# Mixture-of-experts tail of a decoder block: the remaining rows of up to 64 per expert dealt two experts to a tile

## The chip, the cores and the metric

The kernel runs on one core of one Trainium2 chip. A time is the device time of one execution in microseconds (us). The kernel before was run three times: 970.29, 963.82 and 967.57 us, median 967.57. One more execution was profiled; it took 964.87 us, and its span, from the first to the last instruction, is 963.1 us. All durations below come from that execution. Everything is in float32. In the trace, one float32 matrix product stands as two records (two passes over the array), and so does each of its weight loads.

## The reference, cut to what matters

The block is cross-attention followed by a mixture of experts, on 8 x 256 = 2048 tokens of 512 numbers. Only the second half matters here:

```python
h = layernorm(x).reshape(-1, 512)                      # 2048 tokens
scores = softmax(h @ gate_weight.T)                    # 8 experts
topk_w, topk_i = _group_limited_topk(scores)           # best 2 groups of 4, then 2 experts per token
wmat = (one_hot(topk_i, 8) * topk_w[..., None]).sum(1)
g = einsum('th,nfh->ntf', h, gate_w)                   # F = 352
u = einsum('th,nfh->ntf', h, up_w)
e = einsum('ntf,nhf->nth', silu(g) * u, down_w)
routed = einsum('nth,tn->th', e, wmat)
shared = (silu(h @ sh_gate_w.T) * (h @ sh_up_w.T)) @ sh_down_w.T     # F = 704
out = x + routed + shared
```

Each token goes to two of eight experts, so 4096 rows are to be computed by experts. The inputs are fixed by a seed. Evaluated on them, the reference gives the experts 473, 523, 552, 459, 702, 517, 475 and 395 rows.

## The kernel before

Attention, the router and the shared expert are interleaved in `attention` by a hand-written order (`order`, and stages in `Others` that fill the gaps). The PE, ACT, DVE and SP instructions run in exactly the order in which the program issues them; GpSimd's (POOL) order is chosen by a scheduler. For each batch, `router` gives every (token, expert) pair a place in the DRAM table `rows`, and `send` (L961) scatters the normalised tokens there, together with the token's scores and its number. Expert `e` owns the table's rows from `e * S_R` on, with `S_R` = 2176.

After the last batch, `plan` (L969 to L1033) works out on DVE, from the counts, which tiles of 128 rows the experts need. It is 27 DVE instructions, issued back to back. `t_end` (where each expert's rows end) comes first; `t_row` (first row of a tile), `t_exp` (its expert), `t_one` (one-hot of it) and `t_all` (number of tiles) come last. While `plan` runs, PE works through the shared expert of the last batch (`Shared.pieces`, L156). There a result tile `gu` is in one of the three buffers of the PSUM pool `ps_m` (L99), ACT computes the tanh (L176), and two DVE instructions (L177, L178) finish it and release the buffer.

`routed` then computes the experts. The weights of all eight stay in SBUF (`wgu_all`, `wd_all`; 1408 and 768 KB for one expert), loaded by DMAs on SP's queue in the first steps. Tile `i` goes through these functions:

- `load` (L363): SP reads the tile's first row from `t_row` (for `i` >= 8) and starts a DMA of 128 rows into `xs`, which has three buffers.
- `turn` (L368): PE turns the rows with four transposes (`rx`, L372), ACT copies them to `rxT` (L374), DVE picks the weight `rw` and the token numbers `rid` (L376 to L384).
- `up` (L386): PE reads the expert's number from `t_exp` and makes 8 products (`rg`, L393), four for the gate and four for the up projection, each 128 rows of weights by 352 columns; ACT applies silu (L401), DVE multiplies (L403).
- `turn_act` (L405): three transposes (`ra`, L409), two DVE copies to `raT`.
- `down` (L414): 3 products of 512 columns (`ro`, L420), a DVE scaling to `ry` (L428; three buffers), and a scatter by GpSimd that adds the rows to the output (L429).

`run` (L459) is software-pipelined. Step `i` issues load(i + 2), the weights of expert i + 3 while there are any, turn(i + 1), up(i), down(i - 1) and turn_act(i).

Tiles 0 to 7 are the first 128 rows of each expert. For the rest an expert gets whole tiles of 128 rows, the last one partly empty: with the counts above 3, 4, 4, 3, 5, 4, 3 and 3, in sum 29. `N_TILE` = 39 is the most that any routing needs; `N_RUN` = 37 tiles are always computed, so all of 8 + 29 = 37 are filled, and two more stand behind a branch (L485) that is taken if `t_all` says so. Before the experts read their tiles, 8 DMAs write an empty tile (`blank`, L448) behind each expert's last row.

Of the kernel before, what the change touches and what calls it, by code (L numbers as in the profile page):

```python
# [35 lines left out]
F32 = mybir.dt.float32  # L38
I32 = mybir.dt.int32
# [23 lines left out]
S_R = NT + P  # L63
N_TILE = TOP_K * NT // P - 1 + N_EXP
N_RUN = N_TILE - 2
N_PLAN = N_TILE - N_EXP
W = 528
# [9 lines left out]
def xattn_ffn(  # L77
# [35 lines left out]

    blank = dram.tile([P, W], F32, name="blank")
    rows = dram.tile([N_EXP * S_R + P, W], F32, name="rows")
# [217 lines left out]
def routed(ctx, tc, ps_m, wgu, wd, ident, rows, t_exp, t_row, t_one, t_all, t_end, blank, out, tail, right):  # L333
# [11 lines left out]

    def value(table, i, engine, top):
        return nc.values_load(
            table[0:1, i : i + 1],
            engines=(engine,),
            min_val=0,  # L350
            max_val=top,
            skip_runtime_bounds_check_because=because,
        )
# [9 lines left out]
    def load(i):  # L363
        first = i * S_R if i < N_EXP else value(t_row, i - N_EXP, ENG.SP, N_EXP * S_R)
        xs[i] = early.tile([P, W], F32, tag="xs", bufs=3, name=f"xs{i}")
        nc.sync.dma_start(xs[i], rows[bass.ds(first, P), :])

    def turn(i):  # L368
        row = xs.pop(i)
        ps = ps_m.tile([P, NC, P], F32, tag="m", name=f"rx{i}")  # L370
        for c in range(NC):
            nc.tensor.transpose(ps[:, c], row[:, c * P : (c + 1) * P], ident)  # L372
        xTs[i] = early.tile([P, NC, P], F32, tag="xT", name=f"rxT{i}")
        nc.scalar.copy(xTs[i], ps)  # L374

        w1s[i] = early.tile([P, 1], F32, tag="w1", bufs=5, name=f"rw1_{i}")  # L376
        if i < N_EXP:
            nc.vector.tensor_copy(w1s[i], row[:, D + i : D + i + 1])
        else:
            wt = early.tile([P, N_EXP], F32, tag="wt", name=f"rw{i}")  # L380
            nc.vector.tensor_mul(wt, row[:, D : D + N_EXP], t_one[:, i - N_EXP])
            nc.vector.tensor_reduce(w1s[i], wt, AX.X, ALU.add)
        ids[i] = early.tile([P, 1], I32, tag="id", bufs=6, name=f"rid{i}")
        nc.vector.tensor_copy(ids[i], row[:, W_ID : W_ID + 1].bitcast(I32))  # L384

    def up(i):  # L386
# [3 lines left out]
        for k in range(2):  # L390
            for c in range(NC):
                w = wgu_all[:, bass.ds(e, 1), c, k * F : (k + 1) * F]
                nc.tensor.matmul(  # L393
                    gu[k],
                    lhsT=xT[:, c],
                    rhs=w.rearrange("p o f -> p (o f)"),
                    start=(c == 0),
                    stop=(c == NC - 1),
                )
        sg = work.tile([P, F], F32, tag="sg", name=f"rsg{i}")  # L400
# [13 lines left out]
    def down(i):  # L414
        e = exps.pop(i)
        o = ps_y.tile([P, D], F32, tag="y", name=f"ro{i}")
        aT = aTs.pop(i)
        for fc, (_, fn) in enumerate(FCH):
            w = wd_all[:fn, bass.ds(e, 1), fc]
            nc.tensor.matmul(  # L420
                o,
                lhsT=aT[:fn, fc],
                rhs=w.rearrange("p o d -> p (o d)"),
                start=(fc == 0),
                stop=(fc == len(FCH) - 1),
            )
        y = work.tile([P, D], F32, tag="y", bufs=3, name=f"ry{i}")
        nc.vector.tensor_scalar(y, o, w1s.pop(i), None, ALU.mult)  # L428
        nc.gpsimd.indirect_dma_start(  # L429
            out=out,  # L430
            out_offset=bass.IndirectOffsetOnAxis(ap=ids.pop(i), axis=0),
            in_=y,
            in_offset=None,
            compute_op=ALU.add,
        )

# [9 lines left out]
    for e in range(N_EXP):  # L446
        to = value(t_end, e, ENG.SP, N_EXP * S_R)
        alone(tc, nc.sync.dma_start(rows[bass.ds(to, P), :], blank).ins)  # L448
    while tail.cost < 0.8 * tail.total:
        tail.step()  # L450
    turn(0)
    while not tail.over:
# [3 lines left out]
        tc.tile_pool(name="rwork", bufs=2, side="right", reuse_waits="tile")  # L456
    )

    def run(tiles):  # L459

        a, n = tiles[0], tiles[-1] + 1
        for i in range(a, n + 1):
            if a + 3 <= i + 2 < n:
                load(i + 2)
            if i + 3 < N_EXP:
                up_weights(i + 3)
                down_weights(i + 3)
            if i + 1 < n:
                turn(i + 1)
            if i < n:  # L470
                up(i)
            if a < i:
                down(i - 1)
            if i < n:
                turn_act(i)

    run(range(N_RUN))

    filled = nc.values_load(
        t_all[0:1, 0:1],  # L480
        min_val=0,
        max_val=N_PLAN,
        skip_runtime_bounds_check_because=because,
    )
    with tc.If(filled > N_RUN - N_EXP):  # L485
        for i in range(N_RUN, min(N_RUN + 3, N_TILE)):
            load(i)
        turn(N_RUN)
        run(range(N_RUN, N_TILE))


def attention(
# [36 lines left out]
    first = late.tile([P, N_EXP], F32, name="first")  # L529
    nc.vector.tensor_copy(first, numbers[:, :N_EXP])  # L530

    count = late.tile([P, N_EXP], F32, name="count")
# [436 lines left out]
    def plan():  # L969


        behind = late.tile([P, N_EXP], F32, name="behind")
        nc.vector.tensor_add(behind, count, first)
        nc.vector.tensor_copy(t_end, behind)
        n16 = late.tile([P, NTT], F32, name="n16")
        nc.vector.tensor_copy(n16, numbers[:, N_EXP:])
        nc.vector.tensor_scalar(n16, n16, n16[:, 0:1], float(P), ALU.subtract, ALU.add)
        yield 0, False, 0, True

        shape = [P, N_EXP, NTT]  # L980
# [3 lines left out]
            count.unsqueeze(2).to_broadcast(shape),  # L984
            n16.unsqueeze(1).to_broadcast(shape),
            ALU.is_gt,
        )
        tiles = late.tile([P, N_EXP], F32, name="tiles")
        nc.vector.tensor_reduce(tiles, more, AX.X, ALU.add)

        shape = [P, N_EXP, N_EXP]
        upto = late.tile(shape, F32, name="upto")
        nc.vector.tensor_mul(upto, lower, tiles.unsqueeze(1).to_broadcast(shape))
        start = late.tile([P, N_EXP], F32, name="start")
        nc.vector.tensor_reduce(start, upto, AX.X, ALU.add)
        end = late.tile([P, N_EXP], F32, name="end")
        nc.vector.tensor_add(end, start, tiles)
        yield 0, False, 0, True

        nt_i = late.tile([P, N_PLAN], I32, name="nt_i")  # L1000
        nc.gpsimd.iota(nt_i, pattern=[[1, N_PLAN]], base=0, channel_multiplier=0)
        n_t = late.tile([P, N_PLAN], F32, name="n_t")
        nc.vector.tensor_copy(n_t, nt_i)
        shape = [P, N_PLAN, N_EXP]
        mine = n_t.unsqueeze(2).to_broadcast(shape)
        here = small.tile([P, W], F32, tag="row", bufs=4, name="here")
        here = here[:, : N_PLAN * N_EXP].rearrange("p (t e) -> p t e", e=N_EXP)
        nc.vector.tensor_tensor(here, mine, end.unsqueeze(1).to_broadcast(shape), ALU.is_ge)
        e_t = late.tile([P, N_PLAN], F32, name="e_t")
        nc.vector.tensor_reduce(e_t, here, AX.X, ALU.add)  # L1010
        nc.vector.tensor_tensor(t_one, mine, start.unsqueeze(1).to_broadcast(shape), ALU.is_ge)
        nc.vector.tensor_sub(t_one, t_one, here)
        yield 0, False, 0, True

        base = late.tile([P, N_EXP], F32, name="base")
        nc.vector.scalar_tensor_tensor(base, start, float(-P), first, ALU.mult, ALU.add)
        nc.vector.tensor_mul(here, t_one, base.unsqueeze(1).to_broadcast(shape))
        row = late.tile([P, N_PLAN], F32, name="row")
        nc.vector.tensor_reduce(row, here, AX.X, ALU.add)
        nc.vector.scalar_tensor_tensor(row, n_t, float(P), row, ALU.mult, ALU.add)  # L1020
        nc.vector.tensor_scalar(row, row, float(P), None, ALU.add)

        no = late.tile([P, N_PLAN], F32, name="no")
        nc.vector.tensor_scalar(no, e_t, N_EXP - 0.5, None, ALU.is_gt)
        rest = late.tile([P, N_PLAN], F32, name="rest")
        nc.vector.tensor_scalar(rest, row, -1.0, float(N_EXP * S_R), ALU.mult, ALU.add)
        nc.vector.tensor_mul(rest, rest, no)
        nc.vector.tensor_add(row, row, rest)
        nc.vector.tensor_copy(t_row, row)
        nc.vector.tensor_sub(e_t, e_t, no)  # L1030
        nc.vector.tensor_copy(t_exp, e_t)
        nc.vector.tensor_copy(t_all, end[:, N_EXP - 1 :])
        yield 0, False, 0.0  # L1033
# [82 lines left out]
    def transfers():  # L1116
# [8 lines left out]
        nc.sync.dma_start(rows[N_EXP * S_R :, :], empty)  # L1125
        nc.sync.dma_start(blank, empty)
        yield
# [112 lines left out]
```

## Time and profile before

| what | value |
|---|---|
| three runs | 970.29, 963.82, 967.57 us; median 967.57 |
| profiled execution: time, span | 964.87 us, 963.1 us |
| granted TensorE clock, mean | 0.994 |
| PE busy | 939.1 us, 98% of the span |
| DVE, ACT, POOL busy | 456.4, 204.8, 132.4 us |
| routed experts (rg, ro, rx, ra lines of PE) | from about 645 us to about 951 us |
| DMA traffic | 81.79 MB, mean 85 GB/s; about 410 GB/s from 640 to 680 us |

A row of an instruction group reads: line, engine, operation, tile written <- tiles read, count, then busy time and mean duration of one in nanoseconds, then idle time before it with what ended it. PEld is the weight load of PE, which overlaps its products. SPq, ACTq and POOLq are instructions of an engine's sequencer, such as the start of a DMA. Since the passes on PE are pipelined, the distance between two starts tells what a pass costs, not its recorded duration.

### The profile page before, as it was taken

The page shows a single profiled execution, that of the slowest core. Times are in us where ns is not written, and L with a number is a line of the kernel's source. Part 1 is how long each engine was busy: PE and PEld are TensorE (multiplying, and loading weights), DVE is VectorE, ACT ScalarE, POOL GpSimd, SP SyncE. Part 2 cuts the span into 40 slices and gives each one's busy share as a digit, 9 for nine tenths or more (in the row PEclk, how much of TensorE's full clock was granted, in tenths as well). Part 3 has the DMA queues.
Part 4 walks back from the last instruction along what each step waited for, and adds up shares of the span by engine and source line. Part 5 has one row for each costly group of instructions (what it writes and reads, how often), then busy time and mean ns, then how long its engine had stood idle before and what let it go on. Part 6 is the DMA issues. An engine that isn't in the chain of part 4 may idle for free.

```text
span 963.1 us, 12900 instructions
## 1 busy us (share of the span) xinstructions
PE 939.1 (98%) x4981; PEld 559.2 (58%) x4981; DVE 456.4 (47%) x1025; ACT 204.8 (21%) x260; POOL 132.4 (14%) x165
## 2 busy tenths in 40 slices
PE   8999899999999999999999999999999999999994
PEld 8765466446545455664555546675666666666662
DVE  3653756656666666555656635542222222222221
ACT  1223033223323222131232241011111111111110
POOL 3000100211101101100021101110111111111111
PEclk9999999999999999999999999999999999999998
DMA  6368310220111111102011001289833333333322
GB/s 216 93 174 280 93 50 2 73 42 27 46 56 35 46 34 35 41 12 65 3 46 45 33 26 33 89 352 398 283 67 67 67 67 67 67 67 67 67 33 33
DMA packets 37468, 81.79 MB, mean 85 GB/s; under 512 B 6048, under 2 KB 14496, under 8 KB 35872
## 3 DMA queue, kind: packets, MB, share of 16 engines
q1 hardware_dynamic: 28480, 61.50, 20.4%
q0 software_dynamic: 7888, 18.35, 8.7%
q10 hardware_dynamic: 1040, 1.12, 0.4%
q8 instruction: 41, 0.67, 0.3%
q14 instruction: 19, 0.16, 0.1%
HBM read 49.93 MB, written 27.67 MB: 81 GB/s over the span
## 4 chain that ended last, share of the span: by engine, by line
PE 87%; DMA 4%; DVE 3%; SPq 3%; issue 1%; ACT 1%; POOL 1%; ACTq 0%; POOLq 0%; DVEq 0%
PE rg L393 18%; PE gu L164 15%; PE ro L420 10%; PE o L184 9%; PE s L778 6%; PE s L745 6%; PE fc L836 5%; PE av L797 5%; PE pq L711 4%; PE rx L372 2%; SPq L684 2%; DMA rows<-empty 1%; PE ra L409 1%; DVE nm L754 1%; PE pkv L655 1%
## 5 line engine op out<-in xcount | busy, mean ns | idle before, releaser
L754 DVE TENSOR_REDUCE nm<-s 128x8 f32<-128x2048 f32 x64 | 146.5, 2289 | 75.2 <-PE s L745 74.8
L393 PE MATMUL rg<-wgu_all,rxT 128*128 (+1 forms) x592 | 181.3, 459 | 0.0
L786 ACT ACTIVATE ex<-s 128x2048 f32<-128x2048 f32 x64 | 120.1, 1877 | 226.1 <-PE s L778 214.9
L164 PE MATMUL gu<-hT,gu_w 128*128 128x256 f32 x704 | 166.8, 386 | 0.7 <-ACT nmT L766 0.7
L164 PEld LDWEIGHTS gu<-hT,gu_w 128*128 128x128 f32 x704 | 129.0, 190 | 41.7 <-issue 24.1
L393 PEld LDWEIGHTS rg<-wgu_all,rxT 128*128 128x128 f32 x592 | 109.6, 190 | 54.8
L420 PE MATMUL ro<-wd_all,raT 128*128 (+3 forms) x222 | 101.5, 593 | 0.8 <-DVE raT L411 0.8
L429 POOL DMA_INDIRECT y<-ry,rid x37 | 57.4, 1553 | 267.6 <-DVE ry L428 241.2
L184 PE MATMUL o<-down,act 128*128 128x512 f32 x192 | 90.1, 604 | 0.3 <-DVE q L325 0.3
L403 DVE TENSOR_TENSOR ract<-rg,rsg 128x352 f32<-128x352 f32 x37 | 19.4, 524 | 148.6 <-PE rg L393 148.6
L745 PE MATMUL s<-kT,qT 16*128 16x256 f32 x1024 | 74.0, 400 | 3.2 <-DVE nm L754 3.1
L778 PE MATMUL s<-qT,kT 17*128 17x512 f32 x512 | 73.0, 640 | 2.6 <-DVE nm L754 1.8
L420 PEld LDWEIGHTS ro<-wd_all,raT 128*128 128x128 f32 (+1 forms) x222 | 42.2, 190 | 44.1 <-issue 35.4
L745 PEld LDWEIGHTS s<-kT,qT 16*128 16x128 f32 x1024 | 46.7, 184 | 33.8 <-ACT ex L786 14.9
L374 ACT COPY rxT<-rx 128x512 f32<-128x512 f32 x37 | 21.6, 585 | 194.1 <-PE rx L372 194.1
L428 DVE TENSOR_SCALAR ry<-ro,rw 128x512 f32<-128x512 f32 x37 | 27.8, 751 | 74.2 <-PE ro L420 74.2
L711 PE MATMUL pq<-xT,wq_sb 128*128 128x256 f32 x256 | 60.9, 385 | 0.8 <-ACT xT L325 0.8
L836 PE MATMUL fc<-wfc_sb,o 128*128 128x512 f32 x128 | 61.6, 608 | 0.1
L797 PE MATMUL av<-ex,v 128*32 128x512 f32 x512 | 61.5, 598 | 0.0
L961 POOL DMA_INDIRECT rows<-lnf,idx x32 | 31.6, 989 | 208.5 <-DVE idx L955 147.4
L184 PEld LDWEIGHTS o<-down,act 128*128 128x128 f32 x192 | 34.0, 190 | 41.5 <-issue 40.3
L711 PEld LDWEIGHTS pq<-xT,wq_sb 128*128 128x128 f32 x256 | 46.8, 190 | 14.1 <-issue 7.3
(156 smaller groups left out, 691.5 us busy)
## 6 DMA issues: line engine op xcount, KB each, us to landing
wgu_all<-wgu SPq DMA_DIRECT2D x8, 1408.0 KB
xs<-rows SPq DMA_DIRECT2D x37, 264.0 KB
wd_all<-wd SPq DMA_DIRECT2D x8, 768.0 KB
cT<-ctxT SPq DMA_DIRECT2D x8, 512.0 KB
acc<-x SPq DMA_DIRECT2D x16, 256.0 KB
y<-acc SPq DMA_DIRECT2D x16, 256.0 KB
x<-x SPq DMA_DIRECT2D x14, 256.0 KB
qT<-q SPq DMA_DIRECT2D x56, 64.0 KB
```

Of the source, the lines that this page charges most:

```text
L164: nc.tensor.matmul(ps[:, i], lhsT=self.gu[k][:, c, i * P : (i + 1) * P], rhs=hT[:, c], start=(c == 0), stop=(c == NC - 1),)
L184: nc.tensor.matmul(ps, lhsT=act[:, k, q * P : (q + 1) * P], rhs=self.down[:, k], start=(i == 0), stop=(i == len(SCH) - 1),)
L393: nc.tensor.matmul(gu[k], lhsT=xT[:, c], rhs=w.rearrange("p o f -> p (o f)"), start=(c == 0), stop=(c == NC - 1),)
L420: nc.tensor.matmul(o, lhsT=aT[:fn, fc], rhs=w.rearrange("p o d -> p (o d)"), start=(fc == 0), stop=(fc == len(FCH) - 1),)
L429: nc.gpsimd.indirect_dma_start(out=out, out_offset=bass.IndirectOffsetOnAxis(ap=ids.pop(i), axis=0), in_=y, in_offset=None, compute_op=ALU ...
L711: nc.tensor.matmul(ps[:, i], lhsT=wq_sb[:, c, part], rhs=xT[:, c], start=(c == 0), stop=(c == NC - 1),)
L745: nc.tensor.matmul(ps[:, r, j], lhsT=qT[band, G, j0 + j, qc * P : (qc + 1) * P], rhs=kT[band, G], start=True, stop=True,)
L754: nc.vector.tensor_reduce(nms[b, G, j0][:, qc], ps, AX.X, ALU.max, negate=True)
L778: nc.tensor.matmul(ps[:, r], lhsT=kT[band, G, kc * P : (kc + 1) * P], rhs=qT[band, G, j0 : j0 + 2], start=True, stop=True,)
L786: nc.scalar.activation(ex, ps, AF.Exp, scale=HD**-0.5)
L797: nc.tensor.matmul(av[32 * r : 32 * r + 32], lhsT=vs[b % DEEP][:, kc, 4 * G + r], rhs=ex[:, r], start=(kc == 0), stop=(kc == QC - 1),)
L836: nc.tensor.matmul(ps, lhsT=o[:, c, qc * P : (qc + 1) * P], rhs=wfc_sb[:, c], start=(c == 0), stop=(c == NC - 1),)
```

## The change

Rows beyond an expert's first 128 are now planned in two kinds of tile. A full tile has 128 rows of one expert. If 1 to 64 rows remain after an expert's last full tile, they become one half of a half tile: up to two experts share a tile, the first on rows 0 to 63, the second on rows 64 to 127. If 65 or more remain, they make a full tile as before. With the counts above that is 3, 3, 3, 3, 4, 3, 3 and 2 = 24 full tiles and five halves.

`RUN_FULL` = 24 full tiles and `RUN_HALF` = 3 half tiles are always run, so the sequence is 8 + 24 + 3 = 35 tiles, the half tiles at positions 12, 19 and 26 (from 0). Six more full tiles and one half tile stand behind the branch, which is taken if `more > 1`.

In a half tile, every product of `up` and `down` becomes two: rows 0 to 63 with the weights in `wgu_all`/`wd_all`, rows 64 to 127 with a copy of the second expert's weights in `wgu_2`/`wd_2`. Their results go to partitions 0 to 63 and 64 to 127 of the same PSUM tile. The copy is fetched from DRAM by two DMAs on SP's queue (`second`); its buffer is single, so it is refilled three positions after the previous half tile. `load` takes two DMAs of 64 rows for a half tile, and the output scatter becomes two, with two index tiles. `plan` has 39 DVE instructions in place of 27, some constants move from `plan` to GpSimd instructions at the start of the program, and `blank` has 64 rows in place of 128.

```diff
-N_TILE = TOP_K * NT // P - 1 + N_EXP
-N_RUN = N_TILE - 2
-N_PLAN = N_TILE - N_EXP
+R = P // 2
+N_FULL = 30
+N_HALF = N_EXP // 2
+RUN_FULL, RUN_HALF = 24, 3
+N_PLAN = N_FULL + N_HALF
...
     def load(i):
-        first = i * S_R if i < N_EXP else value(t_row, i - N_EXP, ENG.SP, N_EXP * S_R)
         xs[i] = early.tile([P, W], F32, tag="xs", bufs=3, name=f"xs{i}")
-        nc.sync.dma_start(xs[i], rows[bass.ds(first, P), :])
+        k = i - N_EXP
+        step = R if k >= N_FULL else P
+        for p in range(0, P, step):
+            first = i * S_R if k < 0 else value(t_row, k, ENG.SP, N_EXP * S_R, p)
+            nc.sync.dma_start(xs[i][p : p + step], rows[bass.ds(first, step), :])
+
+    def second(i):
+        e = value(t_exp, i - N_EXP, ENG.SP, N_EXP - 1, R)
+        nc.sync.dma_start(wgu_2, wgu[bass.ds(e, 1)].rearrange("o p c f -> p (o c) f"))
+        nc.sync.dma_start(wd_2, wd[bass.ds(e, 1)].rearrange("o p c d -> p (o c) d"))
...
+    def halves(i, w, w_2):
+
+        if i < N_EXP + N_FULL:
+            return [(slice(0, P), w)]
+        return [(slice(0, R), w), (slice(R, P), w_2)]
...
     def up(i):
...
-                nc.tensor.matmul(
-                    gu[k],
-                    lhsT=xT[:, c],
-                    rhs=w.rearrange("p o f -> p (o f)"),
-                    start=(c == 0),
-                    stop=(c == NC - 1),
-                )
+                f = slice(k * F, (k + 1) * F)
+                w = wgu_all[:, bass.ds(e, 1), c, f].rearrange("p o f -> p (o f)")
+                for part, w in halves(i, w, wgu_2[:, c, f]):
+                    nc.tensor.matmul(
+                        gu[k][part],
+                        lhsT=xT[:, c, part],
+                        rhs=w,
+                        start=(c == 0),
+                        stop=(c == NC - 1),
+                    )
...
     def down(i):
...
+            for part, w in halves(i, w, wd_2[:fn, fc]):
+                nc.tensor.matmul(
+                    o[part],
+                    lhsT=aT[:fn, fc, part],
+                    rhs=w,
...
+        for to, (part, _) in zip(ids.pop(i), halves(i, None, None)):
+            nc.gpsimd.indirect_dma_start(
...
+                in_=y[part],
...
     def run(tiles):
...
+        halfs = [n for n, i in enumerate(tiles) if i >= N_EXP + N_FULL]
+        seconds = [0 if len(tiles) < N_EXP else N_EXP - 3, *(n + 3 for n in halfs)]
...
+            for k, at in zip(halfs, seconds):
+                if at == n:
+                    second(tiles[k])
...
+    full = [N_EXP + k for k in range(N_FULL)]
+    half = [N_EXP + N_FULL + k for k in range(N_HALF)]
+    tiles = [*range(N_EXP), *full[:RUN_FULL]]
+    for k in range(RUN_HALF):
+        tiles.insert(N_EXP + 4 + 7 * k, half[k])
+    run(tiles)
...
-    with tc.If(filled > N_RUN - N_EXP):
+    with tc.If(more > 1):
...
     def plan():
...
+        past = late.tile([P, N_EXP], F32, name="past")
+        nc.vector.tensor_scalar(past, full, float(P), float(P), ALU.mult, ALU.add)
+        half = late.tile([P, N_EXP], F32, name="half")
+        nc.vector.tensor_tensor(half, count, past, ALU.is_gt)
+        nc.vector.tensor_add(past, past, first)
+        h_start, h_end = upto(half, "h")
...
+        for name, sl, start, end, base in (
+            ("f", slice(0, N_FULL), start, end, base),
+            ("h", slice(N_FULL, N_PLAN), h_start, h_end, past),
+        ):
...
```

## Prediction

> **What bounds the kernel now.** I read the page first, for the engine that ends last, then the stage of the routed experts by windows, then single tiles.
>
> ```profile
> PE 939.1 (98%) x4981; PEld 559.2 (58%) x4981; DVE 456.4 (47%) x1025; ACT 204.8 (21%) x260; POOL 132.4 (14%) x165
> PE 87%; DMA 4%; DVE 3%; SPq 3%; issue 1%; ACT 1%; POOL 1%; ACTq 0%; POOLq 0%; DVEq 0%
> ```
>
> PE is busy 98% of the span and holds 87% of the chain that ended last. So time is saved only where PE work goes or a PE wait goes, and added where PE gets work or a wait. The windows of the experts' stage (columns: length, then busy time of PE, PEld, DVE, ACT, POOL, granted clock, DMA share, GB/s):
>
> ```profile
> 660.00:680.00 20.00, 20.00 (x71) 11.99 (x70) 4.37 (x13) 2.56 (x5) 3.19 (x2) 1.00 1.02 409
> 700.00:750.00 50.00, 50.00 (x181) 30.39 (x180) 12.58 (x42) 6.76 (x13) 9.45 (x7) 1.00 0.35 70
> ```
>
> PE never pauses, whether the DMA engines are full (weights arriving, 409 GB/s) or nearly idle; all other engines have room. The price of a tile is the distance of two equal ACT instructions in the timeline, first in the full stretch, then in the quiet one:
>
> ```profile
> 666.05 0.58 ACT L374 COPY rxT<-rx 128x512 f32<-128x512 f32 x1 [5.30 <-PE rx L372]
> 674.13 0.58 ACT L374 COPY rxT<-rx 128x512 f32<-128x512 f32 x1 [5.30 <-PE rx L372]
> ...
> 771.08 0.58 ACT L374 COPY rxT<-rx 128x512 f32<-128x512 f32 x1 [5.30 <-PE rx L372]
> 779.16 0.58 ACT L374 COPY rxT<-rx 128x512 f32<-128x512 f32 x1 [5.30 <-PE rx L372]
> ```
>
> A tile costs 8.08 us in both. The chain near the end shows what it consists of (start, length, what, passes):
>
> ```profile
> 940.21 4.74 PE rg L393 x16
> 944.94 2.59 PE ro L420 x6
> ```
>
> That is 0.296 us for a pass of 352 columns and 0.43 us for one of 512; the rest of 8.08, 0.75 us, is seven transposes.
>
> **The change, part by part.**
>
> (1) *Tiles that go.* With the counts of the inputs, 37 tiles become 35: 29 full tiles behind the first eight become 24 full and three half tiles. If a half tile costs a full one's time, 2 x 8.08 = 16.16 us go.
>
> (2) *What a half tile costs on PE.* It has 16 + 6 products in place of 8 + 3, each with 64 columns of weights. No product with 64 columns is in the trace. The nearest row is attention's `av` (L797): four products, each on its own 32 columns of the array with its own weights and its own moving data. PE's timeline around one such group:
>
> ```profile
> 84.37 1.14 PE L778 MATMUL s<-qT,kT 17*128 17x512 f32 x8
> 85.44 1.93 PE L797 MATMUL av<-ex,v 128*32 128x512 f32 x16
> 87.30 0.66 PE L629 MATMUL tx<-ident,x 128*128 128x128 f32 x4
> ```
>
> From 85.44 to 87.30 are 1.86 us for 16 passes of 512 columns. One after the other they would take 16 x 0.43 = 6.9 us; four abreast 4 x 0.43 = 1.72. So they run abreast, accumulation over two rounds included, and the group pays 0.14 us once. The score group before it takes 85.44 - 84.37 = 1.07 us for two slots (0.86), so 0.21 us of entry and exit. Bounds: a half tile's 22 passes per half run fully abreast (7.31 us, as a full tile; less is excluded, since the moving columns are the same), or one after the other (+7.31 us a tile, +21.9 us for three). I take abreast, the value of the nearest row, plus 0.2 us for each change of layout group: `up` and `down` of three half tiles are six groups, +1.2 us. [...]
>
> (3) *The longer plan.* 27 DVE instructions run from 625.71 to 632.12 us, ahead of the shared expert's DVE work:
>
> ```profile
> 625.71 0.16 DVE L973 TENSOR_TENSOR behind<-count,first 128x8 f32<-128x8 f32 x1
> ...
> 632.06 0.14 DVE L1032 CAST t_all<-end 128x1 int32<-128x1 f32 x1
> 632.12 0.41 DVE L177 SCALAR_TENSOR_TENSOR sg<-sg,gu 128x256 f32<-128x256 f32 x1
> 632.57 0.42 DVE L178 SCALAR_TENSOR_TENSOR act<-sg,gu 128x256 f32<-128x256 f32 x1
> ```
>
> There are 39 after, in the same place. The 12 extra are small; small ones here start 0.1 to 0.26 us apart, so +1.2 to +3.1, and adding the new list up by its neighbours' spacings gives +2.1 us. Who waits: L178 releases a PSUM buffer at 632.99. The chain has PE on `gu` at that time:
>
> ```profile
> 622.83 17.47 PE gu L164 x80
> ```
>
> 80 passes in 17.47 are 0.218 each, so the fourth `gu` tile, which needs the buffer of the first, begins at 622.83 + 48 x 0.218 = 633.3. Now it has 0.3 us of slack; with +2.1 us, PE stalls 1.8 us (0.9 to 2.8). Later tiles find their buffers free, since DVE works off the queue faster than PE fills it. PE is the bound from there on, so this is lost for good.
>
> (4) *Copies of weights.* Three times 1408 + 768 KB on SP's queue, about 5.3 us each at 410 GB/s. The first starts at step 5 behind the last expert's weights and is needed at position 12 (some 56 us later); the next two start at positions 15 and 22 and are needed four tiles (32 us) later. SP spends most of a tile waiting in front of a load (min, median, max in ns):
>
> ```profile
> L366 SPq EVENT_SEMAPHORE  x40: 17/7200/7367, 633.5 to 902.0; - x40
> ```
>
> and the scatter L429, though it takes up to 10.6 us to land while the DMA engines are full, held no tile up:
>
> ```profile
> DMA to landing us min/median/max: 4.7/5.1/10.6
> ```
>
> The copy's wait for `down` of the previous half tile holds SP back by `up` + `down`, under 8 us, and what is queued behind it, the load of `xs` for a later tile, is asked for about 24 us ahead. Cost 0; without that cover, up to 5.3 us each.
>
> (5) *Two scatters for a half tile.* Each waits for the one before to land: 2 x (0.5 + 5.1) = 11.2 us in place of 8.08, so GpSimd falls 3 us behind and catches up by 2.5 us a tile; `ry` is three deep (16 us of cover). Cost 0. The extra 0.14 us index copy on DVE lies in its idle 37 of 50 us.
>
> (6) *Start of the program.* Six more GpSimd instructions of 0.1 to 0.18 us come ahead of the first `rstda`, which had no idle time before it:
>
> ```profile
> 7.38 0.72 POOL L617 TENSOR_TENSOR rstda<-rstda,mhalf 128x2 f32<-128x2 f32 x1
> ...
> 11.39 1.04 PE L629 MATMUL tx<-ident,x 128*128 128x128 f32 x8
> ```
>
> About 0.8 us later, the centred tokens are there at 9.9 in place of 9.1 us; PE turns them at 11.39, after the projections of the context. Cost 0; 0.8 us without that cover. Half-size blanks take about 1 MB (2.6 us of DMA) out of the full stretch, where PE does not wait: 0.
>
> Sum: -16.16 + 1.2 + 1.8 = -13.2 us. On the profiled execution 964.87 becomes 951.7. Its time lies 2.7 us below the median of the three runs; on the mean of all four (966.6) it becomes 953.4, which I forecast. A measurement of this kernel tells about 1% (9.7 us) from no change; the forecast is 1.4%.
>
> **The rivals** (times on 964.87).
>
> *The halves run one after the other.* Then a half tile costs 14.6 us: -13.2 + 21.9 = +8.7, 973.6, slower. For it: no 64-column row exists, and the two products of a pair alternate between weights addressed by a register and fixed ones. Against it: `av`. It decides from where a half pass costs more than 13.2 / 66 = 0.20 us beyond its share.
>
> *Every pair drains.* If each of 22 slots, not each group, pays the 0.14 us that an `av` group pays once, three tiles cost +9.2 - 1.2: 959.7, within 1%. Against it: `av` has four slots and pays once. [...]
>
> *Copies collide with scatters.* If each copy holds one scatter at 10.6 us beyond `ry`'s cover, a tile waits 10.6 - 8.08 = 2.5 us, three +7.6: 959.3. Against it: between 660 and 680 us just that happened, and tiles kept 8.08.
>
> *The branch is taken.* The counts give exactly 24 full tiles, the limit; an expert with 62 rows left turns that into a 25th from three rows more. Then seven tiles and at least a load come on top: above 951.7 + 7 x 8.08 = 1008. The chip would have to choose differently from the reference for three tokens of one expert.
>
> *No stall from the plan:* 949.9, inside the forecast.
>
> **How the numbers follow.** Forecast 0.82; pairs drain 0.07; one after the other 0.06; copies collide 0.03; branch 0.02. The likeliest time is 953.4 us. Its own range is 949 to 958: the stall's bounds, and a spread of the runs before of 6.5 us. To 8 in 10 I take 948 to 961, which takes in the draining and the colliding case. Faster by over 1%: 0.78 (the forecast less 0.04 for its upper edge); within 1%: 0.14 (that 0.04, draining, half of the colliding and a quarter of the serial case); slower by over 1%: 0.08 (the branch, the rest of the serial and colliding cases, which lie near 1%).
>
> **What would show it.** Right: 35 `rxT` copies with steps of 8.1 us, and about 8.3 to 8.5 us around positions 12, 19 and 26; 32 passes of a half tile's `up` in 4.8 to 4.9 us; one idle gap of PE of 1 to 3 us near 633 us, released by DVE; no PE wait on a DMA. Wrong: `up` of a half tile near 9.5 us (serial) or 7 us (drains), a PE wait on `xs` or `wgu_2`, DVE waiting for `ry`, no gap at 633 us, or more than 35 tiles.

## The result, and the profile after

The changed kernel took 958.90 us in the median of five runs (953.48 to 960.36), the kernel before, beside it, 967.15 us. The ratio is 0.9909 with a 95% interval of 0.9883 to 0.9934: faster by 0.9%. One execution was profiled: 959.21 us, 5.66 us less than the profiled execution of the kernel before (964.87); its span is 957.4 us. The forecast was 953.4 us and the sum behind it -13.2 us. So the sign was right and the time lies inside the range, but of the gain 8.25 us arrived between the medians, and less than half on the profiled executions.

The page, first its engines, then its chain:

```profile
PE 926.7 (97%) x4989; PEld 545.7 (57%) x4989; DVE 455.5 (48%) x1026; ACT 202.9 (21%) x256; POOL 134.0 (14%) x171
PE 84%; DMA 4%; DVE 4%; SPq 3%; issue 1%; ACT 1%; POOL 1%; ACTq 0%; POOLq 0%; DVEq 0%
```

PE was busy 12.4 us less, but the span fell by 5.7 only: 6.7 us of PE idle time are new. To find them I cut the span at events that both kernels have. The steps of the experts' tiles, in the timeline of ACT (start, length):

```profile
742.71 0.59 ACT L390 COPY rxT<-rx 128x512 f32<-128x512 f32 x1 [5.30 <-PE rx L388]
750.79 0.59 ACT L390 COPY rxT<-rx 128x512 f32<-128x512 f32 x1 [5.30 <-PE rx L388]
759.21 0.59 ACT L390 COPY rxT<-rx 128x512 f32<-128x512 f32 x1 [5.49 <-PE rx L388]
767.59 0.59 ACT L390 COPY rxT<-rx 128x512 f32<-128x512 f32 x1 [5.60 <-PE rx L388]
775.67 0.59 ACT L390 COPY rxT<-rx 128x512 f32<-128x512 f32 x1 [5.30 <-PE rx L388]
```

There are 35 of these copies. From the third tile on all steps are 8.08 us, but for two at each half tile, 8.42 and 8.38: 0.64 us for one half tile. The chain shows where (start, length, what, passes), the half tile's `up` first:

```profile
750.70 4.88 PE rg L421 x32
755.58 2.78 PE ro L449 x6
759.12 4.74 PE rg L421 x16
763.86 2.73 PE ro L449 x12
```

The 32 passes of 64 columns take 4.88 us, 0.14 more than 16 full ones, and the full tile's `ro` behind them takes 2.78 in place of 2.58, since its first weight load is no longer hidden: it starts at 755.51 us, with the product that needs it, where that of the full tile before starts 0.30 us ahead of its product (746.89 and 747.19). With the half tile's own `ro` (2.73) and what follows it, a layout group costs about 0.32 us.

The stall from the plan is there. DVE, and PE with its wait in brackets:

```profile
627.46 0.16 DVE L1037 TENSOR_TENSOR behind<-count,first 128x8 f32<-128x8 f32 x1
...
636.04 0.18 DVE L1119 CAST t_row<-row 128x34 int32<-128x34 f32 x1
636.14 0.41 DVE L185 SCALAR_TENSOR_TENSOR sg<-sg,gu 128x256 f32<-128x256 f32 x1
636.59 0.42 DVE L186 SCALAR_TENSOR_TENSOR act<-sg,gu 128x256 f32<-128x256 f32 x1
```

```profile
624.53 10.63 PE L172 MATMUL gu<-hT,gu_w 128*128 128x256 f32 x48
637.06 7.17 PE L172 MATMUL gu<-hT,gu_w 128*128 128x256 f32 x32 [1.91 <-DVE act L186]
```

L186 lets the buffer go at 637.01, and PE starts its fourth `gu` tile at 637.06. From the first plan instruction to this release are 9.55 us, against 7.28 before (625.71 to 632.99), so the plan is 2.27 us longer. The 80 `gu` passes and the wait take 19.54 us (624.53 to 644.07) where they took 17.37: 2.17 us lost.

What the prediction did not have is at the end of the program. From the start of the last scatter to the end of the span the kernel before needs 8.73 us (954.37 to 963.1) and the changed one 13.36 us (944.04 to 957.4). GpSimd's sequencer in the line of the branch, and in the program's last line (count, shortest/median/longest ns, first and last start), before:

```profile
L485 POOLq EVENT_SEMAPHORE  x1: 17/17/17, 954.9 to 954.9; - x1
L485 POOLq INC_SWDGE_SEM  x1: 1559/1559/1559, 955.0 to 955.0; - x1
L1236 POOLq DRAIN  x3: 51/107/5697, 956.6 to 962.8; - x3
```

and after:

```profile
L532 POOLq EVENT_SEMAPHORE  x4: 17/42/43, 944.6 to 949.1; - x4
L532 POOLq INC_SWDGE_SEM  x1: 1571/1571/1571, 949.2 to 949.2; - x1
L1323 POOLq DRAIN  x3: 51/107/5778, 950.8 to 957.1; - x3
```

The branch is not taken in either kernel. When GpSimd skips it, it still waits for semaphores (four such instructions in place of one), then does one instruction of 1.6 us, then a drain of 5.7 us. Before, the instruction of 1.6 us starts 0.6 us after the last scatter's start, and both lie at least in part beside the scatter's transfer. After, it starts at 949.2, when the last scatter has landed (948.9): everything comes behind it. The records of these waits say which semaphores. The last scatter signals number 115 in the kernel before, and the skipped branch there waits for 116 and 117. In the changed kernel the last scatter signals 116, and the branch waits for all of 111 to 118. The branch's body issues two scatters in the kernel before (two tiles), and eight in the changed one (six full tiles, and a half tile with two), and the scatters of either kernel signal eight semaphores in turn, 111 to 118.

The difference of the profiled executions, by these cuts: two tiles -16.16, six layout groups +1.92, plan +2.19, end of program +4.63, and +1.75 that is there before the plan begins. Sum -5.67 us; measured -5.66.

The +1.75 does not show as a cost of the change. In the five profiled executions of the kernel before and its variants below, `t_end` is written at 624.4 to 629.0 us, in the seven of the changed kernel and its variants at 623.9 to 628.3 us; only a cost that is small beside this spread could hide in it. A part of the spread is the clock. The windows (length, busy time of PE, PEld, DVE, ACT, POOL, granted clock, DMA share, GB/s) around a pause of PE of 3.11 us that both kernels have at 111 to 114 us, before:

```profile
114.00:121.00 7.00, 6.50 (x36) 3.87 (x36) 4.82 (x7) 0.36 (x1) 1.02 (x5) 0.76 0.00 1
```

and after:

```profile
114.00:121.00 7.00, 6.80 (x27) 4.31 (x28) 4.08 (x6) 0.36 (x1) 0.52 (x1) 0.52 0.00 1
```

The clock falls to half for 3.4 us in the one and for 6.8 us in the other. In the twelve profiled executions of this study it did so for 0, 3.4 or 6.8 us, in kernels that are nearly alike up to there. The plan's `t_end` came at 624.2 us in the mean of the two executions with none (623.9 and 624.4), at 626.2 in that of the six with 3.4 us (624.6 to 628.0) and at 628.2 in that of the four with 6.8 us (627.7 to 629.0).

### The profile page after: what moved, and what is told of

Same layout as the page of the kernel before. It is cut to its first block, busy times and chain, and to the rows that moved or that the text cites. A ratio compares the mean times of both kernels' runs of the same rounds, so it can differ in the third digit from the quotient of the medians.

```text
span 957.4 us, 12926 instructions
## 1 busy us (share of the span) xinstructions
PE 926.7 (97%) x4989; PEld 545.7 (57%) x4989; DVE 455.5 (48%) x1026; ACT 202.9 (21%) x256; POOL 134.0 (14%) x171
## 4 chain that ended last, share of the span: by engine, by line
PE 84%; DMA 4%; DVE 4%; SPq 3%; issue 1%; ACT 1%; POOL 1%; ACTq 0%; POOLq 0%; DVEq 0%
PE rg L421 17%; PE gu L172 14%; PE ro L449 9%; PE o L192 9%; PE s L843 6%; PE s L810 6%; PE fc L901 5%; PE av L862 5%; PE pq L776 4%; PE rx L388 2%; DMA rows<-empty 1%; DVE nm L819 1%; PE ra L437 1%; SPq L749 1%; SPq L791 1%
## 5 line engine op out<-in xcount | busy, mean ns | idle before, releaser
L421 PE MATMUL rg<-wgu_all,rxT 128*128 (+2 forms) x560 | 171.6, 459 | 0.0
L421 PEld LDWEIGHTS rg<-wgu_all,rxT 128*128 128x128 f32 (+1 forms) x560 | 101.1, 186 | 54.3 <-issue 6.9
L449 PE MATMUL ro<-wd_all,raT 128*128 (+5 forms) x210 | 96.5, 595 | 0.8 <-DVE raT L439 0.8
L449 PEld LDWEIGHTS ro<-wd_all,raT 128*128 128x128 f32 (+3 forms) x210 | 38.4, 186 | 44.2 <-issue 37.1
```

The lines of the kernel that those rows point to most:

```text
L421: nc.tensor.matmul(gu[k][part], lhsT=xT[:, c, part], rhs=w, start=(c == 0), stop=(c == NC - 1),)
L449: nc.tensor.matmul(o[part], lhsT=aT[:fn, fc, part], rhs=w, start=(fc == 0), stop=(fc == len(FCH) - 1),)
```

## The experiments

Each was timed against the kernel before (967.86, 967.72 and 966.23 us in the three series); the ratio is to it. "The end" is from the start of the last scatter to the end of the span in the profile.

**One tile fewer behind the branch.**

```diff
-N_FULL = 30
+N_FULL = 29
```

> One full tile fewer stands behind the branch (N_FULL 29 in place of 30), so its body has seven scatters in place of eight; the branch is still not taken and the 35 computed tiles are the same. Theory (the end): when the branch is skipped, GpSimd makes up for the semaphores of the body's scatters, and with eight scatters these include that of the last scatter before the branch, so it waits for that one to land. With seven it needn't: the time from the start of the last scatter to the end of the span goes from 13.3 us back to about 9 us (8.7 in the kernel before), the whole execution about 4.3 us below the changed kernel. Rival (the size of the body: more instructions to jump over): one of seven tiles is taken out, so at most a seventh of 4.6 us, 0.7 us, is gained, and the end stays at 12.6 us or more.

Measured: 954.96 us, ratio 0.9858 (0.9829 to 0.9886), profiled 955.61. The end is 9.04 us. GpSimd's sequencer in the line of the branch:

```profile
L532 POOLq EVENT_SEMAPHORE  x3: 43/43/43, 945.2 to 945.4; - x3
L532 POOLq INC_SWDGE_SEM  x1: 1586/1586/1586, 945.5 to 945.5; - x1
```

With seven scatters in the body, the records show waits for seven semaphores, all but that of the last scatter (116). The instruction of 1.6 us now starts 0.8 us after the scatter's start (944.68), nearly as in the kernel before. A tile that never runs cost 4.3 us. This version covers every routing but those that need 30 full tiles (nearly all rows on the same two or three experts).

**The plan in pieces.** DVE's plan is cut, and two instructions of the shared expert's stage go between the pieces.

```diff
-    others.finish(others.add(plan(), 1.0, 0, 1))
+    planned = others.add(plan(), 1.0, 0, 1)
+    for steps in (2, 1):
+        for _ in range(steps):
+            planned.step()
+        for _ in range(4):
+            shared[-1].step()
+    while not planned.over:
+        planned.step()
```

> The same 39 instructions of the plan, but the DVE work of the first two gu tiles of the last batch is issued between them in place of behind them. Theory (the longer plan holds a PSUM buffer): PE's idle gap of 1.9 us ahead of the fourth gu tile is gone, PE runs 80 gu passes without a break in about 17.5 us, the experts start 2.2 us earlier, and the whole execution is about 2.2 us below the changed kernel; what the plan releases later (the first weights on SP's queue, about 1.8 us later) costs nothing. Rival (the gap only moves: PE waits for weights or rows of the first experts that start later): the first rxT copies come no earlier, and the time stays.

Measured: 953.72 us, ratio 0.9858 (0.9834 to 0.9882), profiled 952.89. PE's timeline:

```profile
620.79 17.53 PE L172 MATMUL gu<-hT,gu_w 128*128 128x256 f32 x80
```

All 80 passes are in one piece, with no wait: 17.37 us to the next group, as before. From `t_end` to the experts' first transpose copy are 20.03 us (623.92 to 643.95), 2.2 less than in the changed kernel (22.21, 627.65 to 649.86) and as much as before the change (20.02, 625.90 to 645.92). That is the stall. The profile's total fell by 6.3 us, more than the stall; 3.7 of it come from before the plan, where this execution had no half-clock stretch at all (granted clock 1.00 from 110 to 128 us).

**Half tiles computed as full ones.**

```diff
-                for part, w in halves(i, w, wgu_2[:, c, f]):
+                for part, w in [(slice(0, P), w)]:
...
-            for part, w in halves(i, w, wd_2[:fn, fc]):
+            for part, w in [(slice(0, P), w)]:
```

> In the half tiles, up and down make one product of 128 columns with the first expert's weights in place of two of 64; the second expert's weights are still copied but not used, so rows 64 to 127 are computed with the wrong expert. Everything else is as in the changed kernel. Theory (a group of paired products pays about 0.34 us once, for the drains and for weight loads that a drain exposes): the steps around a half tile go from 8.42 and 8.38 us to 8.08, 1.9 us in all, and nothing else moves. Rival (the halves themselves run slower than a full product, or the copies of weights or the second scatter cost the tile's time): the steps stay above 8.08 us.

Measured: 956.98 us, ratio 0.9891 (0.9865 to 0.9918), profiled 956.82. The steps around the same half tile:

```profile
750.84 0.59 ACT L390 COPY rxT<-rx 128x512 f32<-128x512 f32 x1 [5.30 <-PE rx L388]
758.92 0.59 ACT L390 COPY rxT<-rx 128x512 f32<-128x512 f32 x1 [5.30 <-PE rx L388]
767.00 0.59 ACT L390 COPY rxT<-rx 128x512 f32<-128x512 f32 x1 [5.30 <-PE rx L388]
```

All steps are 8.08. So the 0.64 us of a half tile come from its 64-column products alone; the copies of the weights, the two loads and the two scatters, which are still there, cost nothing. This run does not use the copied weights, so a copy need not wait until the products of the previous half tile have read them. In the changed kernel two copies wait for that, 9.9 us in all, but PE waits there in the experts' stage only in the first tile and in the last (0.7 and 0.8 us), as before the change, so that wait costs nothing either.

**The products of one half first, then those of the other.** The order within `up` and `down` of a half tile changes, nothing else.

```diff
-            for c in range(NC):
+            for n, (part, _) in enumerate(halves(i, None, None)):
+                for c in range(NC):
```

> The same products, but within a half tile all of the first half's come first, and then all of the second half's, in place of alternating. Theory (PE starts products in the order of the program, and two run abreast only if neighbours in that order use different columns): up of a half tile takes about 9.5 us in place of 4.8 and down 5.1 in place of 2.6, so three half tiles cost 3 x 7.3 = 22 us more, about 980 us. Rival (a product for free columns is started ahead of the waiting ones, so the order doesn't matter): the time stays at 959.

Measured, one run: 963.83 us. A half tile costs 2.26 us more than in the changed kernel (steps of 9.77 and 9.29 us), 6.8 us for three, and not 22. My reason for that number fell: PE does not work through the products of the two halves one by one in the order of the program. The program has four gate products (8 passes) on the first half's columns (`wgu_all`), four on the second's (`wgu`), then the same for the up projection. PE's timeline:

```profile
749.10 1.69 PE L421 MATMUL rg<-wgu_all,rxT 128*64 x5
750.34 0.51 PE L421 MATMUL rg<-wgu,rxT 128*64 128x352 f32 x1
750.63 0.46 PE L421 MATMUL rg<-wgu_all,rxT 128*64 x1
...
751.58 0.51 PE L421 MATMUL rg<-wgu_all,rxT 128*64 x1
...
752.46 0.46 PE L421 MATMUL rg<-wgu,rxT 128*64 128x352 f32 x1
```

The second half starts at 750.34, when the first is four passes of its eight ahead (1.24 us), and from then on both run. At 751.58 the first half begins its up products, while the second half's gate products, which stand before them in the program, go on; the last of their passes starts at 752.46. So the up product of the first half starts 0.88 us before the last gate pass of the second half: products on different columns did not start here in the order of the program. The lead is paid once per group: four passes of 0.296 us in `up` and two of 0.43 us in `down`, 2.0 of the 2.26 us.

**The kernel before with eight scatters behind its branch**, by six more tiles that never run:

```diff
 N_RUN = N_TILE - 2
+N_TILE += 6
```

> The kernel before, with eight tiles in place of two behind its branch (never taken with these inputs). Theory (the end): eight scatters behind the branch use all eight semaphores, so the skipping path waits for the last scatter to land, and the time from the start of the last scatter to the end of the span goes from 8.7 to about 13.3 us: 4.6 us slower, plus some 0.3 us for the longer tables of the plan if they reach past the 0.3 us of slack. Rival (the longer end comes from something else in the change, such as the half tiles' scatters or the copies): it stays at 8.7 us.

Measured: 968.42 us, ratio 1.0021 (1.0000 to 1.0042). In the profile the end is 13.17 us in place of 8.73, as expected; the time grew by less than that, 2.0 us by the ratio and 0.7 us between the medians. This was repeated, below.

**The changed kernel without the branch.** Its line and body are left out, so a routing that needs more tiles would lose rows.

> The changed kernel without its branch: the six full tiles and the half tile that other inputs would need are left out. Theory (the end is the skipping path's bookkeeping behind the last scatter): from the start of the last scatter to the end of the span about 7 us, its landing of 5 us and the closing barrier, 6 us below the changed kernel. Rival (the long GpSimd drain of 5.7 us at the end is the price of any scatter, not of the bookkeeping): about 8.7 us or more as in the kernel before, at most 4.6 us gained.

Measured: 953.08 us, ratio 0.9868 (0.9844 to 0.9892), profiled 952.95. The end is 8.51 us, not 7. The rival was right on that part: the drain is there without the branch. Its record then starts at 942.51, 0.2 us before that of the last scatter, and ends 7.9 us later. The gain at the end is 4.85 us.

**The kernel before without its branch**, in the same way.

> The kernel before without its branch (the two tiles that other inputs would need are left out). The same end as in the changed kernel without its branch is expected: about 7 us from the start of the last scatter in place of 8.7, so 1.7 us faster. Against the changed kernel without its branch this gives the change with no branch in either: 16.2 us of tiles less 1.9 (half tiles) and 2.2 (plan), 12 us; if more is missing, a further cost lies elsewhere.

Measured: 966.63 us, ratio 0.9992 (0.9973 to 1.0011), end 8.23 us and again not 7. So the branch of the kernel before costs 0.5 us at the end, which the timing can't tell from nothing. With no branch in either, the change saves 11.4 us on the profiled executions (964.31 to 952.95) and 13.6 on the medians, where 12 were expected, so no further cost shows.

**Both mends together**: `N_FULL` = 29 and the plan in pieces.

> The changed kernel with both repairs, seven scatters behind the branch (29 full tiles at most in place of 30) and the plan mixed with the last batch's DVE work. If the two terms are independent, 4.3 + 2.2 = 6.5 us below the changed kernel, near 952.4 us against its median of 958.9, a ratio of about 0.985 to the kernel before. Rival (the gains overlap or one of them only moves): 955 us or more.

Measured: 951.74 us (948.06 to 955.62), ratio 0.9843 (0.9815 to 0.9870), end 9.04 us, 20.03 us from `t_end` to the experts. In the profile both terms are gone together, 4.3 and 2.2 us, and the time is near the 952.4 us expected for their sum. This version has the lowest median, with the limit of the first one; its interval overlaps those of the versions with one of the two, so the timing alone does not show that the gains add.

**The kernel before with seven, and again with eight.** As above, with `N_TILE += 5` and `N_TILE += 6`.

> The kernel before with five more tiles behind the skipped branch, so that its body holds seven scatters (one fewer than in the earlier run with eight), tables five entries longer. Theory (the skipped branch waits for the semaphore of the last scatter only if the body uses all eight semaphores): the end stays as in the kernel before, 8.7 to 9.1 us from the start of the last scatter to the end of the span, and the time is that of the kernel before plus some 0.3 us for the longer tables, ratio 1.000 to 1.001. Rival (each scatter of the body costs GpSimd or the branch some time, whichever semaphore it uses): the end grows with the number, 8.73 + 5/6 of 4.4 = 12.4 us, ratio about 1.004.

> The kernel before with six more tiles behind the skipped branch once more, beside the one with five, since its time (ratio 1.0021, interval 1.0000 to 1.0042) was less than its profile's end (13.17 us in place of 8.73) asks for. Theory: end 13.2 us again, and against the run with seven scatters +4.1 to +4.4 us, ratio to the kernel before 1.004 to 1.005. Rival (the wait at the end costs only part of that in a run without a profile): the end is 13.2 us in the profile, but the time is within 2 us of that with seven scatters.

Measured: with seven 967.36 us, ratio 1.0001 (0.9988 to 1.0014), end 8.94 us; with eight 970.25 us, ratio 1.0043 (1.0028 to 1.0058), end 13.06 us. The sequencer in the line of the branch, with seven:

```profile
L486 POOLq INC_SWDGE_SEM  x1: 1566/1566/1566, 958.3 to 958.3; - x1
```

and with eight:

```profile
L486 POOLq INC_SWDGE_SEM  x1: 1551/1551/1551, 958.2 to 958.2; - x1
```

Their last scatters start at 957.48 and 953.26, so this instruction comes 0.8 us behind the one and 5.0 us behind the other. By the ratios, five more tiles cost nothing that the timing can tell and the sixth 0.42%, 4.1 us, as much as the end grew (13.06 less 8.94); between the medians it is 2.9 us. The cost is a step that comes with the eighth scatter, and it is not part of the half tiles at all. The first run with eight gave a smaller ratio; the two intervals overlap. The longer end stands in every profile with eight scatters; how much of it the time shows is less certain.

## Why the prediction was right, and where it was off

- *The bound and the tiles.* Right. PE sets the time in the experts' stage, and 35 tiles at 8.08 us in place of 37 gave the 16.16 us.
- *The halves run abreast.* Right: 32 passes in 4.88 us, against 4.7 if fully abreast and 9.5 in sequence. The rivals "one after the other" and "every pair drains" are out.
- *A change of layout group, 0.2 us.* Mis-sized: 0.32 us, 1.92 in place of 1.2 us for six, of which the third experiment removed all. The `av` and score rows gave the entry and exit of groups, but in the experts' tiles the first weight load of the full products behind a group also lies open: `ro` 2.78 in place of 2.58 us. That the array drains at such a change, or at every pair, is an assumption of mine: no record of PE shows it there, the runs show the time alone.
- *The plan, +1.8 us.* Right in place and cause, one gap released by L186 at 637 us; 2.2 us in size. The 12 instructions took 2.27 us and not 2.1, and the slack was 0.24 us (the fourth tile began at 633.23, the buffer came free at 632.99) and not 0.3. PE started 0.05 us after the release, and its first pass then took 0.32 us, 0.10 more than the others. The second experiment removed it all.
- *Copies and scatters, 0; start of the program, 0.* The first two shown by the third experiment: with copies and scatters in place and no 64-column products, every step is 8.08. (With KB of 1024 bytes a copy is an estimated 5.4 us at 410 GB/s, and not 5.3.) The start was not tested by itself.
- *The end of the program.* This is the step that failed. The sum ended with the last tile and took the time behind it as unchanged, 11.6 us from PE's last product to the end before and 16.1 after. I weighed the branch only as taken or not taken. The trace of before already shows that GpSimd, when it skips the branch, waits for one semaphore for each scatter of its body (two), out of eight in use, and how long it takes from the last scatter to the end; the eight scatters of the new body can be counted in the changed program. In the forecast's terms: -13.2 + 4.6 (end) + 0.7 (layout) + 0.4 (plan) = -7.5 us. The measured ratio asks for -8.8 us (-6.4 to -11.3), and the profiled pair, less the 1.75 us from ahead of the plan, for -7.4.
- *The chances.* The forecast had 0.78 on faster by over 1%; it became 0.9%, with an interval from 0.7 to 1.2%. What took it there was none of the rivals named. The forecast's own range, 949 to 958 us, was missed by 0.9 us. That 948 to 961 held was luck in part: its upper edge was set for draining and colliding, neither of which came, and it covered a cost that nobody had put into it.

## What to carry to other kernels

A branch that is never taken can still be work at the place where it is skipped: here the end took 13.36 us with eight scatters in its body and 9.04 with seven. List what each engine waits for on the skip path, and see that it does not include the transfer that ends last. Here one tile less in the body, never run, was worth as much as half of a real one. Where the last engine's work becomes shorter, follow the program to its very end before adding up, and where a stage of small instructions stands ahead of a buffer's release, deal it out in pieces between the releases.

## What the runs showed of the hardware

- Products on different columns of the array overtook each other in the run with one half first. With products of the two halves in blocks (four in `up`, three in `down`), the half that stood behind started four passes late in `up` (1.24 us) and two passes late in `down` (0.91 us, 763.61 to 764.52), not a block late, and PE began a later product of one half 0.88 us before the last pass of an earlier one of the other.
- Near 112 us PE pauses, for 1.7 to 4.2 us in eleven of the twelve profiled executions and for less than 0.8 us in one. Behind the pause the granted clock was 0.5 for 0, 3.4 or 6.8 us, and the length of the pause alone does not settle which: behind 3.11 us it was 3.4 us in the kernel before and 6.8 us in the changed one, behind 1.73 us it was 3.4 us (the kernel before without its branch), behind 2.15 us none (the first run with eight). The clock records have the stretch as 3.413 us in the kernel before (116.07 to 119.48 us) and as 6.827 us in the changed one (114.22 to 121.05). What sets its length was not tested. Pause and clock together are a reason why two profiled executions could not tell a microsecond or two here.
- GpSimd's long drain at the program's end takes 5.7 to 5.8 us where it starts behind the bookkeeping of the branch, whether the last scatter has landed by then (the changed kernel) or not (the kernel before: 956.58 against 959.07 us). Without a branch, its record starts 0.2 us before that of the last scatter and takes 7.6 us (the kernel before) and 7.9 us (the changed one). What it waits for was not tested.
